# Row sums of the first adjacency: 16 TensorE products with ones replaced by eight ScalarE sums and two small transfers

## The chip, the cores and the metric

The kernel runs on one core of one Trainium2 chip. The metric is the device time in microseconds (us) of one execution. A core has five engines that matter here: PE (TensorE, matrix products; PEld is its weight load), DVE (VectorE), ACT (ScalarE), POOL (GpSimd) and SP (SyncE, which here only issues transfers). PE writes its sums into PSUM, from where ACT or DVE carries them to SBUF. Each engine executes its own instructions in order and waits for the others by semaphores.

## The reference

There are B = 16 graphs with N = 1024 nodes and C = 128 features, each with a symmetric 0/1 adjacency. A gated layer (four steps of a GRU over aggregated neighbours) is followed by a convolution layer of four rounds, each ending with a normalisation over all graphs and nodes:

```python
def _L1_gnn_ref(x, adj, W, b, gamma, beta):
    h = x
    for i in range(4):
        h = jnp.einsum('bnm,bmc->bnc', adj, h @ W[i]) + b[i]
        h = jax.nn.relu(h)
        mu = jnp.mean(h, axis=(0, 1))
        var = jnp.mean(jnp.square(h - mu), axis=(0, 1))
        h = gamma[i] * (h - mu) * jax.lax.rsqrt(var + EPS) + beta[i]
    return h

h = jnp.maximum(_layernorm(x), 0.0)
x = x + gated(h, adj, nodemask, ...)          # four steps: m = adj^T (h W); h = GRU(m, h)
h = jnp.maximum(_layernorm(x), 0.0)
x = x + _L1_gnn_ref(h, adj, ...)
```

In rounds 1 to 3 the kernel starts graph 0 before the mean and variance of the round before are known: it aggregates the raw values, and repairs the result afterwards with scale and shift. The shift is multiplied by the row sum of graph 0's adjacency (its `degree`). This row sum is what the change computes differently.

## The kernel before, in words

**Gated layer.** Two graphs are in flight, streams `sa` (even graphs) and `sb` (odd graphs). One half-step makes the gates of one stream (`products`, `reset_gate`, `candidate`, `update_gate`) and the aggregation of the other (`agg_step`, 32 products of 128x512). The order on every engine is written out by hand in `half_step`; `clock` counts the half-steps, the first one under `first_step` being 3. Extra work is put into an agenda with `at(n, place, go)`, and `due(place)` runs it when the half-step with number n comes to that place: "start", "beside0" and "beside1" (after the reset gate of half 0 or 1, before its tanh, L1016), "mid" (behind half 0, through `mids`, which first has POOL copy a `pace` column that waits for half 0), "gap" (behind half 1, before the aggregation is issued), "end". In half-steps 3 to 5 a layer's weights are turned as well: `turn_ih` (L475 to L481: PE transposes, one ACT copy to `w_both`) and `join_layer` (L486: a product that reads `w_both`, placed in the middle of the aggregation).

The adjacency rows of a graph are eight tiles of 128x1024 in fp32r, `sa.rows` and `sb.rows`. Graph 0 uses its rows in four aggregations, the last of them in half-step 7; in half-step 8 POOL begins to write the rows of graph 2 into the same buffers. `glance` (L586) is an ACT activation over a whole row tile with an accumulated sum, which later half-steps use for another purpose.

**Convolution.** For each graph, `load_adjT` reads eight bf16 tiles (`block` for even graphs, `packed` for odd ones; SP issues them) and DVE (L1313) or ACT (every third from row 1, L1311) widens each to fp32r, `wide`, in a ring of 12 buffers. `aggregate` (L524) makes 32 products with the two parts of the features, `chw`. In round 0 these come by `first_split`: a load on POOL's queue (L1368), an ACT copy (L1370) and a DVE subtraction (L1371); `first_weights` then copies the sums (`cm`, L1380) and makes four products (L1381). This part is not ordered by hand: a planner places its instructions by program order and its own costs. The order in time can thus differ from that of the program.

**The row sums.** In round 0, behind graph 0's aggregation, `row_sums` multiplies a 128x128 tile of ones with the eight widened tiles, 16 products into two PSUM tiles (`pt_deg`, L1407), and two ACT copies (L1411) carry the result, the same in all 128 partitions, to `degree`. `degree` is the space of `w_mT`, a weight tile of the gated layer that nothing reads after its last gates. The reader is `raw_weights` (L1398), in rounds 1 to 3.

Of the kernel before, what the change touches and what calls it, by code (L numbers as in the profile page):

```python
# [8 lines left out]
F32 = mybir.dt.float32  # L9
F32R = mybir.dt.float32r  # L10
BF16 = mybir.dt.bfloat16
U16 = mybir.dt.uint16
I32 = mybir.dt.int32
AF = mybir.ActivationFunctionType
ALU = mybir.AluOpType
AX = mybir.AxisListType
P = 128
HALF = 512
# [323 lines left out]
def exact_path(  # L342
# [21 lines left out]
    nc = tc.nc  # L364
    B, N, C = x.shape
    L = g_weight.shape[0]
    NB = N // P
    NH = N // HALF
# [3 lines left out]
    const = ctx.enter_context(tc.tile_pool(name="const", bufs=1))  # L372
    small = ctx.enter_context(tc.tile_pool(name="small", bufs=2))
    dram = ctx.enter_context(tc.tile_pool(name="dram", bufs=1, space=bass.MemoryType.DRAM))
# [7 lines left out]
    def tmp(name):  # L382
        return ps_t.tile([P, HALF], F32, tag="tmp", name=name)

    adjT_d = [dram.tile([NB, P, N], BF16, tag=f"adjT{b}", name=f"adjT_d{b}") for b in range(B)]
    xmid_d = [dram.tile([N, C], F32, tag=f"xmid{b}", name=f"xmid_d{b}") for b in range(B)]
    ymid_d = [dram.tile([P, N], F32, tag=f"ymid{b}", name=f"ymid_d{b}") for b in range(B)]
# [20 lines left out]
    nc.vector.memset(eps_t, EPS)  # L408
    ones = const.tile([P, 1], F32, tag="ones", name="ones")
    nc.vector.memset(ones, 1.0)  # L410
    low = const.tile([P, (B + 2) * NB], F32, tag="low", name="low")
    nc.vector.memset(low, 0.0)

# [52 lines left out]
    def turn_hh(i):  # L466

        pt = tmp(f"pt_whh{i}")
        for g in range(3):
            nc.tensor.transpose(pt[:, g * P : (g + 1) * P], wns["hh", i][:, g, :], ident)  # L470
        nc.scalar.copy(w_hhT[:, i, :], pt[:, : 3 * P])

    def turn_ih(prep, w_g, i):

        pt = tmp(f"pt_wih{i}")  # L475
        for g in range(3):
            nc.tensor.transpose(pt[:, g * P : (g + 1) * P], wns["ih", i][:, g, :], ident)
        nc.tensor.transpose(pt[:, 3 * P :], w_g[:, i, :], ident)
        both = prep.tile([P, 4 * C], F32, tag="w_both", name=f"w_both{i}", bufs=1)
        nc.scalar.copy(both, pt)  # L480
        turned[i] = both[:, 3 * C :], both[:, : 3 * C]  # L481

    def join_layer(i):
        w_gT, w_ihT = turned[i]
        pw = tmp(f"pt_wm{i}")
        nc.tensor.matmul(pw[:, : 3 * P], w_gT, w_ihT, start=True, stop=True)  # L486
        nc.scalar.copy(w_mT[:, i, :], pw[:, : 3 * P])
# [29 lines left out]
    def aggregate(pm, hw, rows, g):  # L517
        aggregate_rows(pm, hw, rows, range(g * BH, (g + 1) * BH))
# [14 lines left out]
    with ExitStack() as st:  # L533
        work = st.enter_context(tc.tile_pool(name="work", bufs=2))
# [45 lines left out]
        def glance(b, stage, js):  # L580

            junk = work.tile([P, N], BF16, tag="junk", name=f"junk{b}_{js[0]}", bufs=1)
            for j in js:
                lows = stage[j % 4].bitcast(U16).rearrange("p (n t) -> p n t", t=2)[:, :, 0]
                k = b * NB + j
                nc.scalar.activation(junk, lows, AF.Copy, accum_out=low[:, k : k + 1])  # L586

        def exchange_out(t, name, d=None):
            if d is None:
                d = rawd.tile([P, HALF], F32, tag="cross", name=f"cross_{name}", bufs=8)  # L590
            nc.sync.dma_start(d, t)
            return d
# [25 lines left out]
        def transposes(batches):  # L618

            for b, rows in batches:  # L620
                adjT = turned_tile(f"adjT{b}")
                ahead = transpose_rows(b, rows[0], 0, adjT)
                for j in range(NB):
                    go = ahead
                    if j + 1 < NB:
                        ahead = transpose_rows(b, rows[j + 1], j + 1, adjT)
                    go()
                    yield j
                nc.gpsimd.dma_start(adjT_d[b].rearrange("k p n -> p k n"), adjT)
                yield NB  # L630
# [428 lines left out]
        def at(n, place, go):  # L1059
            agenda.setdefault((n, place), []).append(go)  # L1060
# [5 lines left out]
        def first_step(one, two, gated, halfway):  # L1066

            feed.next_step()
            if one is sa:
                feed.jobs = transposes([(s.b, s.rows) for s in (sa, sb)])  # L1070
            one.split_step()
            feed.some(2)
            two.gate_step(0)
            two.half_away(0)
            if feed.full or (clock[0], "mid") in agenda:
                mids(two)
            feed.some(1)
            two.gate_step(1)
            two.half_away(1)
            gated()  # L1080
            one.agg_step(0)
            halfway()
            feed.some(NB if one is sa else 1)
            one.agg_step(1)
            two.finish()
            clock[0] += 1

        def mids(two):

            pace = small.tile([P, 1], F32, tag="pace", name=f"pace{clock[0]}")  # L1090
            nc.gpsimd.tensor_copy(pace, two.new[:, :1])
            feed.store()
            due("mid")
# [58 lines left out]
        sa, sb = Stream(0), Stream(1)  # L1152
        every = {getattr(mybir.EngineType, e) for e in ("PE", "DVE", "Activation", "Pool", "SP")}
        prep = st.enter_context(tc.tile_pool(name="prep", bufs=1))
        with tc.manual_schedule(engines=every):
# [111 lines left out]
            def ahead(i):  # L1267
                join_layer(i)
                if i + 1 < L:
                    turn_hh(i + 1)  # L1270

            sa.plan(0)
            sb.plan(1)
            first_step(sa, sb, looks, lambda: ahead(1))
            first_step(sb, sa, lambda: turn_ih(prep, w_g, 2), lambda: ahead(2))
            written[0] = False
# [23 lines left out]
    work = ctx.enter_context(tc.tile_pool(name="work2", bufs=2))  # L1300
    feat = [feat_pool.tile([P, N], F32, tag=f"f{b}", name=f"feat{b}") for b in range(B)]

    def load_adjT(b, i):
        ts = []
        block = None if b % 2 else turned_tile(f"block{b}_{i}")
        for j in range(NB):
            t = half_tile(f"packed{b}_{i}_{j}") if b % 2 else block[:, j, :]
            nc.sync.dma_start(t, adjT_d[b][j])
            r = row_tile(f"wide{b}_{i}_{j}")
            if j % 3 == 1:  # L1310
                nc.scalar.copy(r, t)  # L1311
            else:
                nc.vector.tensor_copy(r, t)  # L1313
            ts.append(r)
        return ts
# [38 lines left out]
    def banks(b, i):  # L1354
        return [acc(t, f"pc{b}_{i}_{t}") for t in (("m0", "m1") if b % 2 == 0 else ("g_r", "g_z"))]
# [10 lines left out]
    def first_split(b):  # L1366
        yt = flat(f"y{b}").rearrange("p k c -> p (k c)")
        nc.gpsimd.dma_start(yt, ymid_d[b])  # L1368
        hw = hw_tiles(b, f"chw{b}_0")
        nc.scalar.copy(hw[0], yt)  # L1370
        nc.vector.tensor_sub(hw[1], yt, hw[0].bitcast(F32))  # L1371
        return hw

    def first_weights(b, pm, stats):

        mt = work.tile([P, N], F32, tag="h", name=f"cm{b}", bufs=3)
        pc = [acc(t, f"pw{b}_{t}") for t in ("g_hn", "g_xn")]
        for hf in range(NH):
            cols = slice(hf * HALF, (hf + 1) * HALF)
            nc.scalar.copy(mt[:, cols], pm[hf])  # L1380
            nc.tensor.matmul(pc[hf], w_c[:, 0, :], mt[:, cols], start=True, stop=True)  # L1381
        return conv_done(b, 0, pc, stats)
# [16 lines left out]
            nc.tensor.matmul(pc[hf], w_c[:, i, :], mt[:, cols], start=True, stop=True)  # L1399
        conv_done(0, i, pc, stats)  # L1400

    def row_sums(rows):

        pd = [tmp(f"pt_deg{hf}") for hf in range(NH)]
        for j in range(NB):
            for hf in range(NH):
                nc.tensor.matmul(  # L1407
                    pd[hf], ones_r, rows[j][:, hf * HALF : (hf + 1) * HALF], start=(j == 0), stop=(j == NB - 1)
                )
        for hf in range(NH):  # L1410
            nc.scalar.copy(degree[:, hf * HALF : (hf + 1) * HALF], pd[hf])  # L1411

    xo = []

    def pieces(b):
# [28 lines left out]
            for n0, n in pieces(k):  # L1444
                nc.gpsimd.dma_start(xo_piece(k, n0, n), by_node(xmid_d[k], n0, n))

    ones_r = work.tile([P, P], F32R, tag="ones_r", name="ones_r", bufs=1)
    nc.vector.tensor_copy(ones_r, ones.to_broadcast([P, P]))
    degree = w_mT.rearrange("p l c -> p (l c)")[:, :N]

    stats = small.tile([P, B * NH, 6], F32, tag="bn_st", name="stats0")
# [1 line left out]
    for b in range(B):  # L1453
        rows = load_adjT(b, 0)
        hw_next = first_split(b + 1) if b + 1 < B else None
        pm = banks(b, 0)
        aggregate(pm, hw, rows, 0)
        if waiting:
            last = first_weights(*waiting, stats)
            if b == 1:  # L1460
                with tc.issue_after(last.ins):
                    sb.rest()
        if b == B - 1:
            hw_next = raw_split(1)
        aggregate(pm, hw, rows, 1)
        if b == 0:
            row_sums(rows)
        hw, waiting = hw_next, (b, pm)


# [1 line left out]
    for i in range(1, L):  # L1472
        rows, pm0, hw0 = load_adjT(0, i), banks(0, i), hw
# [8 lines left out]
        for b in range(1, B):  # L1482
            rows = load_adjT(b, i)
# [28 lines left out]
    for b in range(B):  # L1512
# [3 lines left out]
        for n0, n in pieces(b):  # L1516
# [5 lines left out]
            tag = turns[count % len(turns)]  # L1522
# [60 lines left out]
```

## Time and profile before

| | |
|---|---|
| Runs | 1785.47, 1788.07, 1794.2 us; median 1788.07 |
| Profiled execution | 1789.26 us, of which the span of instructions is 1787.5 us |
| PE busy | 1759.3 us, 98% of the span |
| DVE busy | 1305.9 us, 73% |
| ACT busy | 1107.6 us, 62% |
| POOL busy | 379.3 us, 21% |
| Mean granted TensorE clock | 0.999 |
| Gated layer | about the first 1166 us; round 0 of the convolution to about 1320 us |
| Half-steps 5, 6, 7 | start at 79.5, 98.2 and 115.8 us |
| The 16 products with ones | 1178.30 to 1182.2 us |

An engine's busy time says how long it had an instruction in work; the timeline gives start, length, engine, line, output and inputs, and in brackets how long the engine had stood idle and what released it. PE's records overlap: a product of 128x512 is shown with 390 ns, but the next one begins some 230 ns later, so PE's time is read from starts and not from a sum of lengths.

### The profile page before, as it was taken

To read this page: it belongs to the slowest core of one execution; us is meant where nothing else is said; L and a number is where in the kernel's file an instruction comes from. 1 tells how busy PE (TensorE), PEld (TensorE's weight loads), DVE (VectorE), ACT (ScalarE), POOL (GpSimd) and SP (SyncE) were. 2 spreads that over 40 slices of the span, in tenths; PEclk is the share of its full clock that TensorE was granted. 3 is DMA by queue.
4 is the path that set the end of the run, shared out by engine and by line. 5 is a ranking of instruction groups with operands and counts; after the bars stand their busy time and mean duration, and the time that the engine had idled before them with its cause. 6 is when DMAs were issued, how large, how long until landed. Compare 5 with 4: busy or idle time off the path is not lost. (4 is left out here: it accounts for less than half of the span.)

```text
span 1787.5 us, 22335 instructions
## 1 busy us (share of the span) xinstructions
PE 1759.3 (98%) x6734; PEld 1191.7 (67%) x6734; DVE 1305.9 (73%) x2310; ACT 1107.6 (62%) x1713; POOL 379.3 (21%) x417
## 2 busy tenths in 40 slices
PE   9999999999999999999999999999999999999997
PEld 6565655565656565556555556577778888888886
DVE  7677877887887787887797787676666666666665
ACT  5356556556566556665655655476777767768765
POOL 4314323332331331422432333010100000000011
PEclk9999999999999999999999999999999999999999
DMA  7467657777676676776756768788766575767667
GB/s 259 135 175 262 189 163 272 179 208 241 204 200 213 223 212 197 245 202 202 260 169 186 265 174 227 256 287 311 271 228 241 207 253 201 245 224 245 238 217 268
DMA packets 363617, 400.16 MB, mean 224 GB/s; under 512 B 158188, under 2 KB 239888, under 8 KB 363488
## 3 DMA queue, kind: packets, MB, share of 16 engines
q1 hardware_dynamic: 342736, 323.59, 57.6%
q0 software_dynamic: 20224, 74.80, 11.3%
q8 instruction: 55, 0.90, 0.2%
q14 instruction: 74, 0.61, 0.1%
q10 hardware_dynamic: 528, 0.26, 0.0%
HBM read 267.47 MB, written 97.52 MB: 204 GB/s over the span
## 5 line engine op out<-in xcount | busy, mean ns | idle before, releaser
L524 PE MATMUL pm<-row,ghw 128*128 128x512 f32 x2048 | 503.6, 402 | 0.7 <-DVE ghw L926 0.6
L524 PEld LDWEIGHTS pm<-row,ghw 128*128 128x128 f32 x2048 | 383.8, 188 | 106.6 <-issue 29.2
L1016 ACT ACTIVATE r<-r,vecs 128x512 f32<-128x512 f32 x128 | 92.6, 723 | 255.0 <-DVE r L1013 253.1
L524 PE MATMUL pc_m<-wide,chw 128*128 128x512 f32 x1024 | 245.3, 395 | 0.0
L615 POOL CAST half<-row 128x1024 bf16<-128x1024 f32 x128 | 147.4, 1161 | 361.1 <-DMA adjT<-half 347.9
L524 PEld LDWEIGHTS pc_m<-wide,chw 128*128 128x128 f32 x1024 | 190.4, 188 | 41.9 <-issue 3.8
L524 PE MATMUL pc_g_r<-wide,chw 128*128 128x512 f32 x464 | 186.9, 403 | 0.3 <-ACT chw L501 0.3
L524 PE MATMUL pc_g_z<-wide,chw 128*128 128x512 f32 x464 | 181.0, 390 | 0.0
L577 POOL CAST row<-stage 128x1024 fp32r<-128x1024 f32 x112 | 128.6, 1156 | 243.7 <-DMA stage<-in_adj_dram 232.2
L1012 DVE SCALAR_TENSOR_TENSOR r<-g_hn,vecs,r 128x512 f32<-128x512 f32 x128 | 93.3, 729 | 117.9 <-ACT r L1011 66.9
L955 ACT COPY m<-pm 128x512 f32<-128x512 f32 x128 | 68.4, 585 | 163.5 <-PE pm L524 163.5
L1313 DVE CAST wide<-block 128x1024 fp32r<-128x1024 bf16 x160 | 109.9, 692 | 75.5 <-PE pc_m L524 48.3
L1313 DVE CAST wide<-packed 128x1024 fp32r<-128x1024 bf16 x160 | 110.1, 691 | 71.9 <-PE pc_g_z L524 53.5
L1311 ACT CAST wide<-packed 128x1024 fp32r<-128x1024 bf16 x96 | 100.6, 1048 | 58.5 <-PE pc_m L524 29.7
L993 PE MATMUL g_r<-m,w_mT 128*128 128x512 f32 x256 | 132.0, 597 | 3.4 <-ACT m L955 2.9
L1311 ACT CAST wide<-block 128x1024 fp32r<-128x1024 bf16 x96 | 100.7, 1049 | 53.9 <-PE pc_g_z L524 27.7
L993 PE MATMUL g_z<-m,w_mT 128*128 128x512 f32 x256 | 130.7, 592 | 0.0
L993 PE MATMUL g_xn<-m,w_mT 128*128 128x512 f32 x256 | 130.7, 592 | 0.0
L1361 DVE BATCH_NORM_STATS2 stats<-feat 128x6 f32<-128x512 f32 x128 | 84.1, 686 | 47.0 <-ACT feat L1360 45.9
L1029 DVE TENSOR_TENSOR h<-h,r 128x512 f32<-128x512 f32 x96 | 83.8, 872 | 41.9 <-ACT r L1016 41.8
L1033 DVE TENSOR_TENSOR h<-h,z 128x512 f32<-128x512 f32 x128 | 107.8, 842 | 6.8 <-ACT z L1020 0.2
L1011 ACT ACTIVATE r<-g_r,brz 128x512 f32<-128x512 f32 x128 | 87.9, 686 | 39.1 <-PE g_r L993 38.8
(186 smaller groups left out, 2830.5 us busy)
## 6 DMA issues: line engine op xcount, KB each, us to landing
block<-adjT_d SPq DMA_DIRECT2D x256, 256.0 KB, 4.7
packed<-adjT_d SPq DMA_DIRECT2D x256, 256.0 KB, 5.5
stage<-in_adj_dram SPq DMA_DIRECT2D x120, 512.0 KB, 5.7
adjT_d<-adjT POOLq DMA_DIRECT2D x16, 2048.0 KB, 7.7
cross_h<-t_h SPq DMA_DIRECT2D x92, 256.0 KB, 2.2
n_h<-cross_h SPq DMA_DIRECT2D x368, 64.0 KB, 2.0
xmid_d<-x POOLq DMA_DIRECT2D x16, 512.0 KB, 6.9
y<-ymid_d POOLq DMA_DIRECT2D x16, 512.0 KB, 5.4
```

Of the source, the lines that this page charges most:

```text
L524: nc.tensor.matmul(pm[hf], hw[s][:, j * P : (j + 1) * P], rows[j][:, hf * HALF : (hf + 1) * HALF], start=(j == 0 and s == 0), stop=(j == N ...
L577: nc.gpsimd.tensor_copy(t, stage[j % 4])
L615: nc.gpsimd.tensor_copy(t, row.bitcast(F32))
L993: nc.tensor.matmul(po, wT[:, i, g * C : (g + 1) * C], rhs, start=start, stop=stop)
L1011: nc.scalar.activation(r, pr, AF.Sigmoid, bias=brz[:, 3 * i : 3 * i + 1])
L1012: nc.vector.scalar_tensor_tensor(r, phn, b_hn(i), r, ALU.add, ALU.mult)
L1016: nc.scalar.activation(self.r, self.r, AF.Tanh, bias=b_in(self.i))
L1029: nc.vector.tensor_sub(ho, hin, self.r)
L1033: nc.vector.tensor_mul(ho, ho, self.z)
L1311: nc.scalar.copy(r, t)
L1313: nc.vector.tensor_copy(r, t)
L1361: nc.vector.bn_stats(stats[:, b * NH + hf, :], dst)
```

## The change

Three things are edited. The products with ones, their two copies and the tile of ones are taken out. In half-steps 5, 6 and 7 of the gated layer, ACT sums graph 0's eight row tiles along their length into the columns of a small tile `by_row`, one tile in each of four "beside" places and two in each of two "gap" places. In half-step 9 POOL's queue carries `by_row` (128x8) to `degree_d` in HBM, ordered by node, and in round 0, behind graph 2's aggregation in the program, POOL's queue reads these 1024 values into all 128 partitions of `degree`.

```diff
+    degree_d = dram.tile([N], F32, tag="degree", name="degree_d")
...
+    by_row = const.tile([P, NB], F32, tag="by_row", name="by_row")
...
+        def row_sums(rows, js):
+
+            for j in js:
+                junk = work.tile([P, N], BF16, tag="junk", name=f"summed{j}", bufs=1)
+                nc.scalar.activation(junk, rows[j].bitcast(F32), AF.Copy, accum_out=by_row[:, j : j + 1])
...
             sb.plan(1)
+            for n, place, js in (
+                (5, "beside0", (0,)),
+                (5, "beside1", (1,)),
+                (5, "gap", (2, 3)),
+                (6, "beside0", (4,)),
+                (6, "beside1", (5,)),
+                (7, "gap", (6, 7)),
+            ):
+                at(n, place, lambda js=js: row_sums(sa.rows, js))
+            at(9, "mid", lambda: nc.gpsimd.dma_start(degree_d.rearrange("(j p) -> p j", p=P), by_row))
...
-    def row_sums(rows):
-
-        pd = [tmp(f"pt_deg{hf}") for hf in range(NH)]
-        for j in range(NB):
-            for hf in range(NH):
-                nc.tensor.matmul(
-                    pd[hf], ones_r, rows[j][:, hf * HALF : (hf + 1) * HALF], start=(j == 0), stop=(j == NB - 1)
-                )
-        for hf in range(NH):
-            nc.scalar.copy(degree[:, hf * HALF : (hf + 1) * HALF], pd[hf])
...
-    ones_r = work.tile([P, P], F32R, tag="ones_r", name="ones_r", bufs=1)
-    nc.vector.tensor_copy(ones_r, ones.to_broadcast([P, P]))
...
-        if b == 0:
-            row_sums(rows)
+        if b == 2:
+            nc.gpsimd.dma_start(degree, degree_d.partition_broadcast(P))
```

## The prediction

> **What bounds the kernel now.** I read the busy table first, then what PE waits for between the end of the gated layer and the final stage, and then the timelines of the places that the change touches.
>
> ```profile
> PE 1759.3 (98%) x6734; PEld 1191.7 (67%) x6734; DVE 1305.9 (73%) x2310; ACT 1107.6 (62%) x1713; POOL 379.3 (21%) x417
> PE pc_g_r L524 <- ACT chw L501: 0.3, 1, 0.3
> ```
>
> The first line is the page's: PE has 28.2 us without work in the whole span. The second is the whole list of PE's waits from 1166 to 1755 us: one wait of 0.3 us in 589 us. In the convolution, time is PE's time, so a product taken out there is worth what it takes from PE's stream, as long as everyone who supplies PE can be that much earlier. PE's timeline around the products with ones:
>
> ```profile
> 1177.89 0.39 PE L524 MATMUL pc_g_r<-wide,chw 128*128 128x512 f32 x1
> 1178.30 3.91 PE L1407 MATMUL pt_deg<-wide,ones_r 128*128 128x512 f32 x16
> 1182.05 0.39 PE L524 MATMUL pc_g_z<-wide,chw 128*128 128x512 f32 x1
> ```
>
> The reader is to see the starts. From the product before them to the product behind them 4.16 us pass, where two neighbours otherwise begin 0.23 us apart. The 16 products hold PE for 4.16 - 0.23 = **3.93 us**. Sixteen times the 390 ns of a record would be 6.2 us; that counts their overlap twice.
>
> Next, where ACT would do the new sums. These are ACT's waits in half-steps 5 (two lines and its `w_both`), 6 (two lines) and 7 (the copy behind its gap), and the PE weight load that reads `w_both`:
>
> ```profile
> 83.92 0.72 ACT L1016 ACTIVATE r<-r,vecs 128x512 f32<-128x512 f32 x1 [1.82 <-DVE r L1013]
> 89.51 0.72 ACT L1016 ACTIVATE r<-r,vecs 128x512 f32<-128x512 f32 x1 [2.20 <-DVE r L1013]
> 90.71 0.57 ACT L480 COPY w_both<-pt_wih 128x512 f32<-128x512 f32 x1
> 93.69 0.41 PEld L486 LDWEIGHTS pt_wm<-w_both 128*128 128x128 f32 x2
> 102.66 0.72 ACT L1016 ACTIVATE r<-r,vecs 128x512 f32<-128x512 f32 x1 [1.82 <-DVE r L1013]
> 108.89 0.73 ACT L1016 ACTIVATE r<-r,vecs 128x512 f32<-128x512 f32 x1 [2.84 <-DVE r L1013]
> 133.35 1.07 ACT L955 COPY m<-pm 128x512 f32<-128x512 f32 x2 [4.39 <-PE pm L524]
> ```
>
> The bracket ahead of each tanh (L1016) is idle time that a "beside" sum can take: 1.82, 2.20, 1.82 and 2.84 us. The nearest row for such a sum is the glance of later half-steps:
>
> ```profile
> 145.53 1.05 ACT L586 ACTIVATE junk<-stage 128x1024 bf16<-128x1024 uint16 x1
> 146.48 0.19 ACT L586 ACTIVATION_READ_ACCUMULATOR junk<-stage 128x1 f32 x1
> 146.71 1.06 ACT L586 ACTIVATE junk<-stage 128x1024 bf16<-128x1024 uint16 x1
> ```
>
> One costs 1.18 us from start to start, readout of the sum included.
>
> [...] The trace has 1057 ns on 16-bit input; fp32 input with a sum is not in it, and I take the same. [...] the copies at 133.35 us follow a square root with no table load between. [...] the 16 have (3.91 - 0.39) / 15 = 235 ns, and I use the trace. [...] `by_row` goes out as 1024 pieces of 4 bytes; no transfer in this trace is like that.
>
> **The change part by part.**
>
> *Removed.* PE: 3.93 us. ACT: two copies at L1411, 1.06 us from 1182.30. DVE: the ones cast, 0.29 us. Four widening casts had waited for the ones products, 1.9 us together. Of this only PE's part lies on the path; the others only make its suppliers freer.
>
> *Added, four "beside" sums.* Each occupies ACT for 1.18 us, in idle times of at least 1.82 us. At least 0.64 us is left, so the tanh is not later, and nothing behind it on DVE or PE. Cost 0. If fp32 input took double, 2.36 us, three of the four would be late, by 0.54, 0.16 and 0.54 us, together 1.2.
>
> *Two sums in the gap of half-step 5.* Queued behind them on ACT is the copy to `w_both`. It would start at 90.71 + 1.18 + 1.06 = 92.95 instead of 90.71 (a copy can start as the readout starts) and end at 93.52. PE's weight load that reads it began at 93.69: 0.17 us to spare, less the passing of a semaphore. This is the one place in the gated layer with no margin. I take 0.1 us, with 0 and 0.3 as ends. At the double price it would end at 95.9 and PE would wait 2.2 us.
>
> *Two sums in the gap of half-step 7.* They follow the square root and take 2.4 of the 4.39 us in which ACT waits for the aggregation. Cost 0.
>
> *The rows' buffers.* POOL writes graph 2's rows over graph 0's from 140.35 us on; the last sum ends near 131.4. Nobody waits.
>
> *`by_row` out in half-step 9.* That half-step had no "mid" work, so it gains POOL's `pace` copy (about 0.2 us) and the issue. The issue of a 1024-piece load, L539, is 0.9 us. POOL has both in an idle stretch: its casts end at 167.6 and the next begins at 170.75, after waiting 3.18 us for a row. The 1024 pieces are 64 for each of the 16 engines; at 48 ns, the mean packet of queue 1 (57.6% of 16 times 1787.5 us over 342736 packets), about 3 us of each engine, an estimate. They fall together with the loads of graph 3's last four rows (issued at 167.06). The last of these is cast by 178.9, and the aggregation that needs it only begins at 180.2. Cost 0, at the worst 1 us.
>
> *The read into all partitions.* On POOL about 0.55 us like L1368; 128 pieces of 4 KB, 512 KB. Its space is free after 1166.6, its value is written a thousand us earlier, and its reader comes at 1327. Behind it on POOL's queue are the feature loads of later graphs, each one to two graphs ahead of use. But it adds traffic where the transfer engines are full:
>
> ```profile
> 1182.10:1206.00 23.90, 23.90 (x96) 17.59 (x95) 15.22 (x24) 20.00 (x33) 2.63 (x4) 1.00 0.92 322
> ```
>
> This is the stretch behind the products (PE, PEld, DVE, ACT, POOL, clock, DMA share, GB/s). 512 KB at 322 GB/s are 1.6 us of all engines. Twelve widened rows and the bf16 tiles behind them cover that; cost 0, at the worst 1.6.
>
> *The suppliers of the convolution, 3.93 us earlier.* Late next would be graph 3's features:
>
> ```profile
> 1191.62 1.23 DVE L1371 TENSOR_TENSOR chw<-y,chw 128x1024 fp32r<-128x1024 f32 x1 [2.60 <-ACT chw L1370]
> 1197.16 0.39 PE L524 MATMUL pc_g_r<-wide,chw 128*128 128x512 f32 x1
> ```
>
> They are ready at 1192.85 and used at 1197.16, 4.31 us later. After the change PE comes at 1193.23, still 0.38 us behind them even if ACT does not move at all. And ACT does move: it loses 1.06 us of copies, and `first_weights` of graph 0 comes sooner. Rows 4 to 7 of graph 1 (cast from 1176.28 to 1180.1) are first wanted near 1180.1. So I take nothing back here, with 0 to 3.93 as bounds.
>
> **Sum.** -3.93 + 0.1 = -3.8 us: the profiled execution's 1789.26 becomes 1785.4. It lies 1.2 us above the median of the three runs, 1788.07, so against the median the forecast is **1784.3**, 0.2% less. A measurement of this kernel can tell about 0.5% from no change, 8.9 us (its three runs lie 8.7 us apart), so this is "the same".
>
> **The rivals.**
>
> 1. *The gain is lost at the start of the convolution.* In 1182 to 1206 ACT is busy for 20.0 of 23.9 us, with tail work of the last graphs between the casts. If the planner orders ACT otherwise and graph 3's features come later than 1193.2, PE waits for up to the 3.93 us. For: that 0.38 us margin. Against: PE has no wait at all there before, and ACT gets less work. Time 1786 to 1788.
>
> 2. *Slower: the same stretch, with the added transfer in it.* If the 512 KB go in between the feature and row loads at a share of 0.92, those land up to 1.6 us later; with the 3.93 us given back, and ACT's casts behind them, PE ends 1.6 us behind before, 1789.7. It decides when the transfers delay graph 3's or 4's inputs past PE's arrival by more than 3.93 us. Against: only 0.2 us of DVE's casts waited for transfers between 1166 and 1215, so loads are ahead. A double price of the ACT sums (2.2 + 1.2 us) would take back most of the gain, but not more.
>
> 3. *It does more than it says.* The planner might pack the convolution otherwise. PE has 0.3 us of waits there, so beyond 4.2 us nothing is to be had; a time below 1779.1 would have to come from the scatter of runs.
>
> 4. *It does not take PE's time away.* If the products were hidden in a wait of PE, nothing would change: 1788. The timeline shows neighbours on both sides without a wait, which excludes most of it.
>
> **How the numbers follow.** Forecast 0.70, near 1784.3; rivals 1 and 4 together 0.15; rival 2 0.10, half of it with more than I can price; rival 3 with scatter 0.05. The terms reach from -4.2 to +1.6; with some 4 us for the scatter of a median, the range is 1779.5 to 1790. Faster by more than 0.5% (below 1779.1) 0.07, slower by more than 0.5% (above 1797.0) 0.05, the same 0.88.
>
> **What would show it.** Right: no L1407; products of graph 1 spaced 0.23 us through the old place; PE's waits from the gated layer's end to the final stage still below 0.5 us; the eight sums at 1.18 us each; tanh idle times shrunk to about 0.6, 1.0, 0.6 and 1.7 us; PE's `pt_wm` at most 0.3 us late. Wrong: a wait of PE for `chw` or `wide` between 1178 and 1210, half-steps 5 to 10 longer than before, or sums over 1.8 us.

## The result and the profile after

The changed kernel is slower: 1794.43 us (median of 21 runs) against 1790.98 for the kernel before (21 runs), a ratio of **1.002, 95% interval 1.001 to 1.0029**. The profiled execution took 1794.68 us with a span of 1792.9. That is less than the 0.5% that the prediction calls a change, but outside the range given and on the other side of the forecast. The prediction stood on three runs of the kernel before, with a median of 1788.07 us; 21 runs have 1790.98. Of the 10.1 us between the forecast of 1784.3 and the 1794.43 measured, 2.9 are this difference, and the other 7.2 belong to the change.

The removed part brought what was expected, and something that was not in the sum cost more. The busy table of the page of the changed kernel:

```profile
PE 1759.7 (98%) x6718; PEld 1186.9 (66%) x6718; DVE 1299.2 (72%) x2309; ACT 1114.9 (62%) x1727; POOL 380.2 (21%) x420
```

And from its list of what PE waited for over the whole span (engine, line, releaser: total us, times, longest; lines of the gated layer now have numbers 8 higher, L1028 for L1020, L1024 for L1016):

```profile
PE g_z L1001 <- ACT z L1028: 8.8, 15, 1.7
PE pt_wm L488 <- ACT w_both L482: 2.3, 2, 1.6
PE pw_g_hn L1399 <- ACT cm L1398: 0.7, 1, 0.7
```

PE has 16 products fewer and is still not busy for less time; it has 33.2 us without work instead of 28.2. Of the 5.0 us more, 3.9 are in the gated layer. There its busy time grows too, from 1139.1 to 1143.3 us for the same 3663 products: PE's records overlap (in the kernel before, the 16 aggregation products from 51.14 us on take 3.91 us with some 400 ns each, so their starts lie about 235 ns apart), and a short delay between two of them may count as busy. Reading both timelines at the first `m` copy behind each half-step gives the times at which the half-steps end:

| half-step | before, us | after, us | after later by |
|---|---|---|---|
| 4 | 79.46 | 79.84 | 0.38 |
| 5 | 98.20 | 100.77 | 2.57 |
| 8 | 150.92 | 153.99 | 3.07 |
| 21 | 384.20 | 385.09 | 0.89 |
| 22 | 401.77 | 405.18 | 3.41 |
| 37 | 672.34 | 674.27 | 1.93 |
| 38 | 689.91 | 694.46 | 4.55 |
| 53 | 957.71 | 964.07 | 6.36 |
| 54 | 975.28 | 983.30 | 8.02 |
| 64, the last | 1156.20 | 1164.32 | 8.12 |
| end of the span | 1787.5 | 1792.9 | 5.4 |

In these two executions the gated layer loses 8.1 us and the convolution gains 2.7. Part of a loss comes back later (3.07 us at half-step 8, 0.89 at 21), and half-steps 22, 38 and 54 lose 2.5, 2.6 and 1.7 us anew, hundreds of us after the last edit in this layer. So neither the sums nor the small transfer can be the direct cause of these. What goes on all the time shows in the table by stretches, before and then after (us, then busy time and records of PE, PEld, DVE, ACT and POOL, the clock, the share of the transfer engines, GB/s):

```profile
0.00:1160.00 1160.00, 1142.91 (x3673) 684.35 (x3674) 895.72 (x1644) 666.65 (x1153) 351.81 (x371) 1.00 0.69 212
1320.00:1757.00 437.00, 436.64 (x2290) 371.76 (x2289) 283.45 (x449) 308.56 (x387) 11.29 (x20) 1.00 0.65 228
```

```profile
0.00:1160.00 1160.00, 1138.99 (x3641) 677.31 (x3642) 880.69 (x1623) 669.68 (x1162) 350.08 (x372) 1.00 0.76 210
1320.00:1757.00 437.00, 436.64 (x2278) 370.81 (x2277) 283.30 (x445) 311.07 (x390) 11.15 (x20) 1.00 0.66 231
```

In the gated layer the transfer engines are busy for 0.76 instead of 0.69 of the time, for the same GB/s. In the convolution their share hardly changes. The page's lines on SP's queue say the same, before and after: same packets, same bytes, more time.

```profile
q1 hardware_dynamic: 342736, 323.59, 57.6%
```

```profile
q1 hardware_dynamic: 342736, 323.59, 61.2%
```

And the list of issues, again before and after (size, us from issue to landing), shows it in a transfer that never touches HBM, the DMA transpose from SBUF to SBUF:

```profile
adjT<-half SPq DMA_TRANSPOSE x128, 2.8
```

```profile
adjT<-half SPq DMA_TRANSPOSE x128, 3.3
```

What differs for all these transfers is where their tiles lie. `by_row` is a tile of 32 bytes per partition in the first pool, and the tiles allocated behind it in SBUF move by 32 bytes. In the built programs the bf16 rows that the transposes read began at byte 178688 of the partition, a multiple of 256; after the change at 178720. The same holds for `stage`, the exchange tiles and `x`. The engines' own work on shifted tiles hardly changes: by the two pages a tanh has 723 ns before and after, an aggregation product 402 and 403, a widening to bf16 on POOL 1161 and 1164. In HBM the 4 KB of `degree_d` move most later tiles by 4096 bytes.

### The profile page after: what moved, and what is told of

The parts are those of the page before. It is cut to its first block, busy times and chain, and to the rows that moved or that the text cites. A ratio compares the mean times of both kernels' runs of the same rounds, so it can differ in the third digit from the quotient of the medians.

```text
span 1792.9 us, 22314 instructions
## 1 busy us (share of the span) xinstructions
PE 1759.7 (98%) x6718; PEld 1186.9 (66%) x6718; DVE 1299.2 (72%) x2309; ACT 1114.9 (62%) x1727; POOL 380.2 (21%) x420
## 3 DMA queue, kind: packets, MB, share of 16 engines
q1 hardware_dynamic: 342736, 323.59, 61.2%
## 5 line engine op out<-in xcount | busy, mean ns | idle before, releaser
L1024 ACT ACTIVATE r<-r,vecs 128x512 f32<-128x512 f32 x128 | 92.6, 723 | 260.4 <-DVE r L1021 258.8
L1020 DVE SCALAR_TENSOR_TENSOR r<-g_hn,vecs,r 128x512 f32<-128x512 f32 x128 | 93.1, 728 | 97.5 <-ACT r L1019 54.0
L1042 DVE TENSOR_TENSOR h<-h,r 128x512 f32<-128x512 f32 x128 | 111.5, 871 | 4.3
```

Of the source, the lines that this page charges most:

```text
L1020: nc.vector.scalar_tensor_tensor(r, phn, b_hn(i), r, ALU.add, ALU.mult)
L1024: nc.scalar.activation(self.r, self.r, AF.Tanh, bias=b_in(self.i))
L1042: self.last_dve = nc.vector.tensor_add(ho, ho, self.r)
```

## The experiments

Theory A: the 32-byte shift makes transfers slower, and the late transfers stretch half-steps. Theory B: the sums on ScalarE, or the move in HBM, are to blame. The ratios below compare each kernel with the kernel before on the same chip, with 95% intervals.

**The changed kernel, aligned again.** (e1_padded)

```diff
-    by_row = const.tile([P, NB], F32, tag="by_row", name="by_row")
+    by_row = const.tile([P, 8 * NB], F32, tag="by_row", name="by_row")[:, :NB]
```

> The changed kernel with one difference: by_row is taken from a tile of 256 bytes per partition instead of 32, so that every tile allocated behind it in SBUF moves by 256 bytes and not by 32 and starts again at a multiple of 256 as before the change. Theory A (the 32-byte shift makes the transfers slower, and the late transfers make the gated layer's half-steps longer): share of queue 1 back to about 57.6%, the 8 us lost in the gated layer mostly gone, total 2 to 5 us below before, 0.1 to 0.3% faster. Theory B (the sums delay ScalarE's chain, or the HBM addresses moved by 4 KB): nothing changes against the changed kernel, 0.2% slower than before.

Measured: 0.9975 (0.9964 to 0.9985), 1786.7 us. One wider tile takes the kernel from 0.2% slower to 0.25% faster. Queue 1 and the transposes of this kernel:

```profile
q1 hardware_dynamic: 342736, 323.59, 58.3%
adjT<-half SPq DMA_TRANSPOSE x128, 2.8
```

The share is not quite the expected 57.6%, but the other kernels here that keep the alignment have 57.6 to 58.2%. The sums and the move in HBM are still in this kernel, so they can't be the main cause, and theory B falls. The bf16 rows begin at byte 178944, an odd multiple of 256; a multiple of 512 was not needed for the 2.8 us. In its profile the gated layer ends at 1157.08 us, near the 1156.20 of before.

**The shift alone.** (e2_shift32)

```diff
+    pad = const.tile([P, 8], F32, tag="pad", name="pad")
+    nc.vector.memset(pad, 0.0)
     low = const.tile([P, (B + 2) * NB], F32, tag="low", name="low")
```

> The kernel before with nothing but a 32-byte tile (and its memset) at the place of by_row, so that the tiles behind it move by 32 bytes. No sums, no transfer, the products with ones in place. Theory A: slower than before by 5 to 9 us (0.3 to 0.5%), queue 1 at about 61%. Theory B: no change.

Measured: 1.0029 (1.0018 to 1.0039), 1796.96 us, 5 us slower for a tile that nothing uses. Queue 1 and the transposes:

```profile
q1 hardware_dynamic: 342736, 323.59, 60.5%
adjT<-half SPq DMA_TRANSPOSE x128, 3.3
```

**The move in HBM with the small transfer.** (e3_hbm)

```diff
+    degree_d = dram.tile([N], F32, tag="degree", name="degree_d")
...
+            at(9, "mid", lambda: nc.gpsimd.dma_start(degree_d.rearrange("(j p) -> p j", p=P), ident[:, :NB]))
```

> The kernel before with the 4 KB degree_d in HBM ahead of the other HBM tiles and the transfer of 1024 pieces of 4 bytes to it in half-step 9 (its source is a constant, nothing reads it). SBUF stays as before. Theory A: no change, within 1 us. Rival B2 (the move in HBM, or the small transfer, slows the loads): slower by some us, queue 1 above 60%.

Measured: 0.9984 (0.9974 to 0.9993), with queue 1 at 58.0%. Not slower; that half of theory B falls. The slight gain was expected by nobody and led to the run with the transfer alone, below.

**The products alone.** (e4_no_products)

```diff
-        if b == 0:
-            row_sums(rows)
```

> The kernel before without the 16 products with ones and their two copies: degree is left with old weights, so part of the computation is left out. This measures the removed part alone. By the prediction's first step 3.93 us less (0.22%). Rival: suppliers of TensorE can't come earlier, and 0 to 2 us are gained.

Measured: 0.9968 (0.9956 to 0.9979). In its profile the stretch from the last half-step (1161.05 us) to the end of the span (1788.4) takes 627.35 us, before 631.30: 3.95 us less. The 3.93 of the prediction (0.22%) is confirmed there, and the suppliers of PE can all come that much earlier; the ratio alone, 0.21 to 0.44% less, is too wide to tell.

This profile also says how far a single execution can be trusted. Its gated layer is that of the kernel before, with queue 1 at 57.6% and transposes at 2.8 us, and yet it ends 4.85 us later than in the profile of before (1161.05 against 1156.20). So the 8.1 us of the table above does not measure the price of the shift. The ratios over many runs do.

**The transfer alone** (e5_transfer_only), without the move in HBM:

```diff
+            at(9, "mid", lambda: nc.gpsimd.dma_start(out[0][:NB, :].rearrange("j p -> p j"), ident[:, :NB]))
```

> The kernel before with the transfer of 1024 pieces of 4 bytes in half-step 9, here into rows of the output that are overwritten at the end, so that no HBM tile is added and every address stays as before. Against e3_hbm it leaves out the 4 KB move in HBM. Theory H (the move in HBM is what made e3_hbm 0.16% faster): no change against before, or up to 0.1% slower. Theory T (the pace copy and the transfer in half-step 9 did it): 0.1 to 0.2% faster. Theory N (e3_hbm is scatter): no change.

Measured: 0.999 (0.9979 to 1.0001). No cost can be seen. Whether it, the move in HBM or scatter is behind the 0.16% of the run before stays open: the two intervals overlap.

**The sums alone** (e6_sums_only), with a 256-byte `by_row` and the places of the change:

```diff
+    by_row = const.tile([P, 8 * NB], F32, tag="by_row", name="by_row")[:, :NB]
...
+                at(n, place, lambda js=js: sums_of(sa.rows, js))
```

> The kernel before with the eight ScalarE sums at their places, into a 256-byte tile so that alignment is kept; products with ones in place, no transfers, the sums unused. This is the price of the sums alone. By the prediction 0.1 us with ends 0 and 0.3. Rival: by their delays of tanh and of w_both they cost 1 to 3 us.

Measured: 1.001 (1.0 to 1.0019), some 1.8 us by the ratio (the two medians lie 0.3 us apart), more than the 0.1 us that the prediction took, though its interval touches none. In its profile the gated layer ends at 1155.87 us, no later than before, so this one execution does not show where the 1.8 us would be.

**Which tiles.** (e7_shift_work, e8_shift_keep) The shift is given to the gated layer's work pool alone, and then to all the others alone:

```diff
         work = st.enter_context(tc.tile_pool(name="work", bufs=2))
+        off = work.tile([P, 8], F32, tag="off", name="off", bufs=1)
+        nc.vector.memset(off, 0.0)
```

This is the first kernel. The second has 56 columns in this tile, 224 bytes, and the 32-byte `pad` of e2_shift32 ahead of it.

> The kernel before with a 32-byte tile at the head of the gated layer's work pool alone: the bf16 rows from which DMA transposes read, and h, y and m, leave their multiples of 256; the tiles that transfers from HBM and the exchanges of features use (stage, n_h, t_h, x) and the target of the transposes stay aligned. If the transposes' source is what suffers: about +0.3%, as e2_shift32, and transposes land in 3.2 us or more. If the other transfers suffer: no change.

Measured: 1.0022 (1.0013 to 1.0031).

> The complement of e7_shift_work: a 32-byte tile ahead of the long-lived pools and 224 bytes at the head of the work pool, so that stage, n_h, t_h, x and the target of the transposes are off by 32 bytes, and the bf16 source of the transposes, h, y and m are aligned. If the transposes' source is what suffers: no change against before, transposes land in 2.8 us. If the other transfers suffer: about +0.3%.

Measured: 1.0011 (1.0001 to 1.002). The issue lists, first with the work pool shifted, then with the others shifted:

```profile
x<-in_x_dram POOLq DMA_DIRECT2D x14, 512.0 KB, 6.5
adjT<-half SPq DMA_TRANSPOSE x128, 3.4
```

```profile
x<-in_x_dram POOLq DMA_DIRECT2D x14, 512.0 KB, 6.7
adjT<-half SPq DMA_TRANSPOSE x128, 2.9
```

The first kernel comes near the expected 0.3%, within its interval. But the second is not free either, though its interval ends just above none: 0.22 and 0.11% together are about the 0.29% of the whole shift. Queue 1 says the same, with 59.9 and 58.8%, and so does the load of `x`, which takes 6.2 us in the kernel before and 7.1 with the whole shift. Both groups pay. The transposes are slow (3.4 us) when the tile that they read is shifted, and nearly as fast as before (2.9 us against 2.8) when only the tile that they write is.

**How far the shift must go.** (e9_shift64, e10_shift128) The unused tile with 64 bytes and with 128:

```diff
+    pad = const.tile([P, 16], F32, tag="pad", name="pad")
```

The second kernel has 32 columns here.

> As e2_shift32, the kernel before with an unused tile at the place of by_row, here of 64 bytes. If transfers need a start at a multiple of 64, no change against before and queue 1 at 57.6%. If they need 256, slower by about 0.3% as with 32 bytes, queue 1 at about 60%, transposes landing in 3.2 us or more.

Measured: 1.0034 (1.002 to 1.0048).

> The same with 128 bytes. If transfers need a start at a multiple of 128 or less, no change against before. If they need 256, slower by about 0.3%, queue 1 at about 60%.

Measured: 1.0019 (1.0008 to 1.0029). Their queue 1, 64 bytes and then 128:

```profile
q1 hardware_dynamic: 342736, 323.59, 60.4%
```

```profile
q1 hardware_dynamic: 342736, 323.59, 60.2%
```

32, 64 and 128 bytes are all slow (queue 1 at 60.5, 60.4 and 60.2%), 256 is not (58.3% in e1_padded). Between the traces before and after, the mean packet of queue 1 grew from 20.3 to 24.7 ns at 256 bytes, from 29.7 to 32.9 at 512, from 90.9 to 92.2 at 2048 and from 190.3 to 198.5 at 4096. Why a packet takes longer the runs do not show. The rows of whole tiles in the convolution, 2 KB in each partition, pay little: `block` lands in 4.7 us with the 32-byte shift as without, `packed` in 5.7 instead of 5.5, but in 5.7 in the aligned e3_hbm too.

**The two sums ahead of `w_both`** (e11_moved_padded, e12_moved_32), moved from half-step 5's gap to half-step 6's, first in the aligned kernel, then in the changed one:

```diff
-                (5, "gap", (2, 3)),
...
+                (6, "gap", (2, 3)),
```

> e1_padded (256-byte by_row, aligned) with the two sums of half-step 5's gap moved to the gap of half-step 6, away from the copy to w_both that they stand ahead of. If that place costs something even when the transfers are on time, 0.05 to 0.1% faster than e1_padded, about 0.997 of before. If not, 0.9975 as e1_padded.

Measured: 0.9966 (0.9951 to 0.9982), 1783.24 us, the fastest version here; from the 0.9975 of e1_padded it can't be told apart.

> The changed kernel (32-byte by_row, shifted) with the same move. Theory: the late transfers of half-step 5 delay ScalarE, and the two sums then push w_both past TensorE's need, 1.6 us in the changed kernel's profile; moved, this wait goes and the kernel is about 0.1% faster than the changed one, near 1.001 of before, with the shift's cost still in it. If the sums' place doesn't matter: 1.002.

Measured: 1.0012 (1.0003 to 1.002). The wait of PE for `w_both` in half-step 5 is gone from its profile (0.7 us are left, as before, from an earlier half-step). The ratio moves the expected way, by less than the intervals can settle, and the profile shows no gain: in half-step 6 DVE then stands 6.13 us before a late load of `x`, and at the end of half-step 8 this kernel is 3.66 us behind the kernel before, the changed one 3.07. Between the two kernels of this pair lies only the width of `by_row`: 0.46%, 8 us.

## Why the prediction was wrong

**The step that failed** is the sum itself: a term was missing from it, put at nothing without a reason. The change was costed by what its instructions do on each engine and queue, and "The rows' buffers" only asked who waits for a tile. That a new tile moves all those behind it was not asked. Its price is about 5 us alone (the 32-byte pad) and about 8 us in the changed kernel (e11_moved_padded against e12_moved_32), more than the 3.93 us that the products give back. The range was no help: its upper end, 1790, holds the +1.6 us of the added transfer and no scatter, its lower end some 4 us of scatter, and 4 us above 1789.7 would still have been short of 1794.43.

**How the late transfers become time.** Two waits for transfers show it over the whole span, ACT's for the exchanged features `n_h` and DVE's for the input `x` of a coming graph (total us, times, longest). These are the kernels before, after, and after with the wider tile (e1_padded):

```profile
ACT ghw L919 <- DMA n_h<-cross_h: 6.1, 8, 1.5
DVE st_in L664 <- DMA x<-in_x_dram: 15.8, 14, 3.0
```

```profile
ACT ghw L927 <- DMA n_h<-cross_h: 26.4, 18, 3.8
DVE st_in L672 <- DMA x<-in_x_dram: 38.5, 16, 6.2
```

```profile
ACT ghw L927 <- DMA n_h<-cross_h: 10.9, 11, 2.4
DVE st_in L672 <- DMA x<-in_x_dram: 17.1, 14, 3.1
```

All other runs fall in line. The kernels with their tiles at multiples of 256 have 6.1 to 11.5 us for `n_h` and 15.8 to 21.0 for `x`, the ones with the whole shift 23.8 to 28.1 and 35.4 to 38.5, and the two with half of the tiles shifted lie between (19.3 and 28.8, 16.9 and 27.0). PE pays for a part of these waits. One example is half-step 5 on ACT, in the kernel after (the idle time and its releaser in brackets):

```profile
82.38 1.05 ACT L594 ACTIVATE summed<-row 128x1024 bf16<-128x1024 f32 x1
84.30 0.72 ACT L1024 ACTIVATE r<-r,vecs 128x512 f32<-128x512 f32 x1 [0.79 <-DVE r L1021]
87.41 0.62 ACT L927 CAST ghw<-n_h 128x512 fp32r<-128x512 f32 x1 [2.38 <-DMA n_h<-cross_h]
87.94 0.68 ACT L1028 ACTIVATE z<-g_z,brz 128x512 f32<-128x512 f32 x1
95.77 0.57 ACT L482 COPY w_both<-pt_wih 128x512 f32<-128x512 f32 x1
```

The sum itself is done in time; the tanh at 84.30 still waits 0.79 us for DVE. ACT runs in program order (in the trace of after, all 1576 of its activations, copies and casts start in the order of the built program). It stands for 2.38 us before the exchanged features `n_h`, and the gate `z`, queued behind that cast, comes 2.9 us later than before (85.06 us), with everything behind it. The exchange is late because SP's queue is: its first `n_h` load was issued at 78.94 us, before at 76.52, behind transposes at 73.74 (before 71.50). With the shift alone (e2_shift32), ACT waits 2.28 us at the same place, but `w_both` is made at 93.56 us; with the two sums ahead of it, at 95.77. PE then stands still:

```profile
96.39 0.91 PE L488 MATMUL pt_wm<-w_both 128*128 128x384 f32 x2 [1.65 <-ACT w_both L482]
```

The copy ends at 96.34 us and the product starts 0.05 us later. So the place without margin was named rightly, but its margin of 0.17 us was set against transfers that come as before. In e1_padded `w_both` starts at 92.97 us, 0.10 us behind the start of the readout, where the prediction has 92.95, and PE does not wait. Of the 15 waits for `z` in the whole gated layer, 8.8 us, four have the form of half-step 5, with a cast that waited for `n_h` ahead of the gate: 3.1 us, and none of this form before. Ten come from DVE, which let ACT's tanh wait 3.5 to 6.4 us; seven of the eight before (5.0 us in all) are of that kind too. Half-step 22, one of those that lose most, is such a case:

```profile
389.25 0.30 DVE L672 BATCH_NORM_STATS2 st_in<-x 128x6 f32<-128x128 f32 x1 [3.89 <-DMA x<-in_x_dram]
394.00 0.72 ACT L1024 ACTIVATE r<-r,vecs 128x512 f32<-128x512 f32 x1 [6.26 <-DVE r L1021]
395.87 1.12 PE L1001 MATMUL g_z<-h,w_hhT 128*128 128x512 f32 x2 [0.66 <-ACT z L1028]
```

DVE stands before the late `x` with the work of the reset gate queued behind its statistics. It stands so for 6.25, 3.89, 3.67 and 2.98 us in half-steps 6, 22, 38 and 54; before, at the same loads, not at all, 2.40, 0.93 and 0.90.

**What held.** PE's 3.93 us for the products (3.95 measured). The sums' 1.18 us: 1.14 from 82.38 to the end of the readout at 83.52, and 1.23 from one sum to the next in the gap. The "beside" sum of half-step 5 shown above does not delay its tanh. The transfer of 1024 pieces landed after 11.2 us, and no cost of it can be seen. Of the signs of being wrong that the prediction names, one came true: half-step 5 was longer than before, by 2.2 us. **What else was off.** The 3 us of each transfer engine for the 1024 pieces were too high an estimate: the trace has them in 16 packets of 256 bytes, 79 to 282 ns each. The read into all partitions was placed not behind graph 2 but at 1138.4 us, within the gated layer; nothing waited for it visibly. Rival 1 came true in small, though not with graph 3's features: in the changed and the aligned kernel PE waits 0.7 us for `cm` at the start of the convolution (in e4_no_products it does not), and the convolution of e1_padded gains 3.6 us instead of 3.95. Rival 2 had the right sign by another mechanism.

**What stays open.** The ratios of the parts (products 0.9968, shift 1.0029, sums 1.001, transfer 0.999) add up to 0.03% faster, with each interval about 0.1% to either side; 0.2% slower was measured. Four such intervals leave about 0.2% for their sum, an estimate that takes them as independent, so the gap of 0.23% may be scatter. Nor is it settled that the shift costs more in the changed kernel (0.46%) than alone (0.29%); the `w_both` wait was a candidate for it, but with it gone half-step 6 lost 2.7 us instead of 0.5. The read into all partitions has no run of its own. e1_padded, which contains it, is 0.25% faster, and products, sums and transfer without it add up to 0.32%, so a cost beyond the scatter is not seen.

## What to carry to other kernels

Where a kernel's pools are packed one behind the other, a new small tile may not be free: here an unused one of 32 bytes cost 0.29%, and 256 bytes instead of 32 took the change from 1.002 to 0.9975. Pad it so that the tiles that transfers use start at a multiple of 256 bytes where they did so before, and compare the addresses of the built programs before the timelines. A loss that is spread over stages which the edit does not touch, with more share of the transfer engines at the same bytes (here 61.2 for 57.6% on queue 1), is a reason to look at addresses before instructions. And a margin read from one timeline holds only as long as the transfers ahead of it come at the same time: here 0.17 us were counted on, and `n_h` came late enough to hold ACT for 2.38 us.

## What the runs showed of the hardware

- With the bf16 rows, `stage`, the exchange tiles and `x` 32, 64 or 128 bytes off a multiple of 256 in SBUF, queue 1 takes 60.2 to 61.3% of the engines' time instead of 57.6 to 58.3%, for the same 342736 packets.
- The DMA transposes from SBUF to SBUF land in 2.8 us with both tiles at multiples of 256, in 3.4 us with the tile they read 32 bytes off (3.3 with both off), in 2.9 us with only the tile they write off.
- An ACT sum over 128x1024 in fp32 takes 1.05 us and a readout of 0.19 us, as on 16-bit input (1.06 and 0.19); two in a row begin 1.23 us apart, on 16-bit input 1.18.
- 1024 pieces of 4 bytes from SBUF to HBM: 0.89 us of issue on POOL, 10.5 to 11.2 us to landing, 16 packets of 256 bytes in the changed kernel.
